# Queries, keys and two head projections as extra Strassen chunks of a feed-forward matrix, and a memory bank padded to 128 rows

## The chip, the core and the metric

The kernel runs on one core of a Trainium2 chip. The metric is the device time of one execution in microseconds (us). Everything is computed in float32.

## What is computed

x has 8 batches of 1024 tokens with 512 features. Cut to what matters:

```python
xn = layernorm(x)                                     # no scale, no shift
# attention block: four heads of 128 features each, joined by warboss_w
def full(xn, w):                                      # local_qkv_w
    q, k, v = split(xn @ w, 3)
    return softmax(q @ k.T * 128 ** -0.5) @ v
def sparse(xn, w):                                    # sparse_qkv_w: the same, but
    keep = scores >= top_k(scores, 102)[..., -1:]     # only the 102 largest of each row stay
    return softmax(where(keep, scores, -1e9)) @ v
def memory(xn):                                       # bank: 64 x 128
    xp = xn @ memory_proj_w                           # 512 -> 128
    r = softmax(xp @ bank.T) @ bank
    return concat([xp, r]) @ mem_out_w + mem_out_b
def prediction(xn):
    h = xn @ pred_in_w + pred_in_b                    # 512 -> 128
    return gelu(h @ pred1_w + pred1_b) @ pred2_w + pred2_b
s = concat([full, sparse, memory, prediction]) @ warboss_w + warboss_b
# feed-forward: 512 -> 2048 -> 512
g = silu(relu(xn @ ffn_w1 + ffn_b1) @ ffn_w2 + ffn_b2)
out = x + s * g
```

## The kernel before

Two streams of work are woven into one order of instructions.

**The filler** is the feed-forward, `feed_forward`. It takes 512 tokens (a *group* g; two to a batch, 16 in all) at a time through ffn_w1 and 256 tokens (n = 2g, 2g+1) through ffn_w2. Both products are done by Strassen's scheme: of a product of 2 x 2 blocks, seven block products in place of eight. ffn_w1 is cut into eight *up chunks* of 512 rows and 2 x 128 columns, ffn_w2 into eight *down chunks*. A chunk holds seven blocks of 128 x 256 (four raw or summed blocks of the weights among them). In the first group a chunk is loaded from the input, its sums are formed (`form_chunk`: four instructions on DVE for up, on POOL for down), and it is written to DRAM; later groups load it from there as one transfer of 896 KB (`load_chunk`). Four tiles w hold chunks; a chunk is loaded three places ahead of its use and formed one place ahead. The order of the chunks is the list that `plan` yields: eight up chunks of a group with down chunks between them, then eight down chunks, the group's *tail*.

The tokens' side of the first product needs sums too: `token_sums` makes four of them per group on POOL from the transposed tokens xnT. An up chunk then is 7 products of two matmuls with 256 columns each (tile ph), copied out of PSUM by ACT into a tile u with seven slots; `hidden_units` adds the seven into the four results on POOL (`add_products`, five instructions) and ACT writes relu of them into h. An up chunk waits until the units two chunks before it are made.

**The attention** works in *steps* of 128 tokens, eight to a batch. It is written as generators (chains), each of which yields a time or a condition: `local` and `sparse` for the two heads, `sparse_select` for the 102 largest scores (DVE: 13 rounds of eight), `two_heads` for the memory and prediction heads of a pair of steps (256 tokens), `finish_pair` for the join with warboss_w.

**The order.** The program's order is made when the kernel is built: `run` keeps an own clock in matmul columns, lets every chain go on whose time or condition has come, and otherwise takes the next matmul of the filler. A new step is started every STEP columns. Every engine executes its instructions in exactly this order (`InOrder`); SP issues the loads, POOL the constants' loads and nearly all stores.

What the change touches is done directly before, by plain matmuls over four row blocks of 128:

- `project_q` makes q of a pair for both attention heads from a resident matrix w_q: 2 x 4 matmuls of 256 columns (tile pq), started by `next_q` in a step of odd number; ACT scales it into qT (one tile).
- `project_k` makes k of a group and a head: 4 matmuls of 512 columns (tile pk), copied by ACT into kT. In batch 0 it is called while the first tokens are prepared; for later batches `project_keys` loads both matrices (`borrow_qkv`) and calls it for two heads and two groups after the last local scores of the batch before.
- `prediction_head` and `memory_head` begin with 4 matmuls of 256 columns each (tiles ppi, pmp) with matrices that `two_heads` loads for each pair (tile wmp, 2 x 256 KB).
- The memory bank has 64 rows. Its scores (pms) have 64 columns; the weights are transposed to 64 rows (ptm), and the second half of the head's product (pmo, from emT and bank_mo) contracts over 64 rows.

All f32 matmuls appear in the profile as two instructions, each with its load of weights.

Of the kernel before, what the change touches and what calls it, by code (L numbers as in the profile page):

```python
# [20 lines left out]
def kernel(  # L21
# [216 lines left out]
    w_q = const.tile([P, ND, 2, HD], F32, tag="w_q", name="w_q")  # L238
    for h in range(2):
        sp.dma_start(out=w_q[:, :, h, :], in_=qkv[h][:, :HD].rearrange("(c p) n -> p c n", p=P))  # L240
# [8 lines left out]
    brow = sb.tile([NB, P], F32, tag="tmp", name="brow", bufs=3)  # L249
# [5 lines left out]
    bank = const.tile([M, HD], F32, tag="bank", name="bank")  # L255
# [10 lines left out]
    bankT = const.tile([P, M], F32, tag="bankT", name="bankT")  # L266
    bank_mo = const.tile([M, HD], F32, tag="bank_mo", name="bank_mo")
# [5 lines left out]
    def turn_constants():  # L273
        pt = ring("pt_b", (P, 4, P))
        transpose(pt[:, 0, :NB], brow, ident[:NB, :NB])
        transpose(pt[:, 1, :M], bank, ident[:M, :M])
        act.copy(biasT, pt[:, 0, :NB])
        copy(bankT, pt[:, 1, :M], 300)
        yield after("act")
        pt = ring("pt_bm", (P, P))  # L280
        matmul(pt[:M, :], bankT, w_mo[:, 1, :], True, True, HD)
        copy(bank_mo, pt[:M, :], 200)
        done.add("constants")
# [55 lines left out]
    def project_k(b, g, h, w):  # L339
        if b not in kT:  # L340
            kT[b] = sb.tile([P, 2, S], F32, tag="kT", name=f"kT_{b}")
        ps = ring(f"pk_{b}_{g}_{h}", (P, 512))
        accumulate(
            ps,
            [w[:, c, ts(h, HD)] for c in range(ND)],
            [xnT[b, g][:, c, :] for c in range(ND)],
            512,
        )
        copy(kT[b][:, h, ts(g, 512)], ps, 360)
        done.add(("k", b, g, h))  # L350
# [18 lines left out]
    def project_q(b, p):  # L369
        qT[b, p] = sb.tile([P, 2, T], F32, tag="qT", name=f"qT_{b}_{p}")  # L370
        ps = ring(f"pq_{b}_{p}", (P, 2, T))
        for h in range(2):
            accumulate(
                ps[:, h, :], [w_q[:, c, h, :] for c in range(ND)], pair_xnT(b, p), T
            )
        act.activation(qT[b, p], ps, AF.Copy, scale=SCALE)
        on("act", 360)
        done.add(("q", b, p))
# [11 lines left out]
    def plan():  # L390


        half = NWC // 2
        for g in range(GROUPS + 1):
            for k in range(NWC):
                if g < GROUPS:
                    yield "up", g, k
                if k >= half and g < GROUPS:
                    yield "down", 2 * g, k - half
                if k < half and g:  # L400
                    yield "down", 2 * g - 1, k + half
            if g < GROUPS:
                for n in range(2):
                    for k in range(half):
                        yield "down", 2 * g + n, k + half * (1 - n)

# [3 lines left out]
        for kind in ("up", "down")  # L410
        for k in range(NWC)
# [3 lines left out]
    w2v = ffn_w2.rearrange("(h k p) n -> p h k n", h=2, p=P)  # L415

# [4 lines left out]
    raw_blocks = sb.tile([P, 7, H], F32, tag="m", name="raw_blocks")  # L421

    def load_chunk(at):
# [5 lines left out]
        if n:  # L429
            sp.dma_start(out=w, in_=w_dram[kind, k])  # L430
            return
        extra = raw[kind, k] = raw_blocks[:, at % 7]
        if kind == "up":
            for slot, u, h in ((0, 0, 0), (1, 0, 1), (4, 1, 1)):
                sp.dma_start(out=halves(w[:, slot]), in_=w1v[:, h, :, u, k])
            sp.dma_start(out=halves(extra), in_=w1v[:, 0, :, 1, k])
        else:
            for slot, h, d in ((0, 0, 0), (1, 1, 0), (6, 1, 1)):
                sp.dma_start(out=w[:, slot], in_=w2v[:, h, k, ts(d, H)])
            sp.dma_start(out=extra, in_=w2v[:, 0, k, H:])  # L440

    def form_chunk(at):

        if at >= len(order_of_chunks) or order_of_chunks[at][1]:
            return
        kind, n, k = order_of_chunks[at]
        w, extra = w_tiles[kind, n, k], raw.pop((kind, k))
        if kind == "up":
# [4 lines left out]
        else:  # L453
            on_pool("tensor_sub", w[:, 5], extra, w[:, 0])
            on_pool("tensor_sub", w[:, 2], w[:, 6], w[:, 5])
            on_pool("tensor_sub", w[:, 3], w[:, 6], extra)
            on_pool("tensor_sub", w[:, 4], w[:, 1], w[:, 2])
        sp.dma_start(out=w_dram[kind, k], in_=w)
# [29 lines left out]
    def token_sums(g):  # L488

        b, q = divmod(g, NG)  # L490
        if g:
            yield needs(("up", g - 1), *[("xnT", b, 4 * q + j) for j in range(4)])
            yield after("act", 0)
        t = sb.tile([P, 4, 2, T], F32, tag="t", name=f"t_{g}")
# [9 lines left out]
    def hidden_units(g, k, m):  # L504
# [3 lines left out]
        for j, slots in enumerate(((1, 4), (6, 5))):  # L508
            h = sb.tile([P, 2, T], F32, tag=f"h{j}", name=f"h_{2 * g + j}_{k}", bufs=(5, NWC)[j])
            for u in range(2):  # L510
                act.activation(h[:, u], m[:, slots[u]], AF.Relu, bias=bcol(k + NWC * u))
                on("act", 280)
            hidden[2 * g + j, k] = h
        units_made[0] += 1

    units_made = [0]
# [40 lines left out]
    def feed_forward():  # L557

        sums = []
        for at, (kind, n, k) in enumerate(order_of_chunks):  # L560
            if kind == "up":
                wants[0] = lambda: (
                    "constants" in done and n in tokens and units_made[0] > n * NWC + k - 2
# [11 lines left out]
            if kind == "up":  # L575
                m = sb.tile([P, 7, T], F32, tag="u", name=f"u_{n}_{k}", bufs=2)
            elif k == NWC - 1:
                m = sb.tile([P, 7, H], F32, tag="m", name=f"m_{n}")
            for i in range(7):
                if kind == "up":  # L580
                    if i % 2 == 0:
                        ps = ring(f"ph_{n}_{k}_{i}", (P, 2, T))
# [20 lines left out]
                if (i % 2 or i == 6) and (kind == "up" or k == NWC - 1):  # L603
                    a = i - i % 2
                    copy(m[:, a : i + 1], ps[:, : i + 1 - a], 180 * (i + 1 - a))
            if kind == "up":
                start(hidden_units(n, k, m), rank=0)
                if k == NWC - 1:
                    tokens.pop(n)
                    done.add(("up", n))  # L610
                    if n + 1 < GROUPS:
                        start(token_sums(n + 1), rank=0)
# [154 lines left out]
    def tmp(name):  # L767
        return sb.tile([P, T], F32, tag="tmp", name=name, bufs=3)

    def memory_head(b, p, w):  # L770
        n = f"{b}_{p}"
        ps = ring(f"pmp_{n}", (P, T))
        accumulate(ps, [w[:, c, :HD] for c in range(ND)], pair_xnT(b, p), T)
        xp = tmp(f"xp_{n}")
        copy(xp, ps, 220)
        yield after("act")
        ps = ring(f"pms_{n}", (P, 2, M))
        for j in range(2):
            matmul(ps[:, j, :], xp[:, ts(j, P)], bankT, True, True, M)
        e = small.tile([P, 2, M], F32, tag="em", name=f"em_{n}", bufs=1)  # L780
# [21 lines left out]
        for j in range(2):  # L802
            transpose(pt[:M, j, :], e[:, j, :], ident)
        eT = tmp(f"emT_{n}")
        copy(eT[:M, :], pt[:M].rearrange("p j t -> p (j t)"), 220)
        yield after("act")
        ps = ring(f"pmo_{n}", (P, T))
        accumulate(ps, [w_mo[:, 0, :], bank_mo[:M, :]], [xp, eT[:M, :]], T)
# [6 lines left out]
    def prediction_head(b, p, w):  # L815
        n = f"{b}_{p}"
        ps = ring(f"ppi_{n}", (P, T))
        accumulate(ps, [w[:, c, HD:] for c in range(ND)], pair_xnT(b, p), T)
        hi = tmp(f"hi_{n}")
        act.activation(hi, ps, AF.Identity, bias=bcol(B_PI))  # L820
        on("act", 260)
        yield after("act")
# [17 lines left out]
    def finish_pair(b, p):  # L840
# [4 lines left out]
        done.add(("borrowed", b, p))  # L845
# [46 lines left out]
    def prepare_tokens(b):  # L892
        yield needs(("rstd", b))
        for j in range(NT):
            if j == 4:
                yield needs(
                    ("up", (b - 1) * NG), ("head", b - 1, 1, 2), ("head", b - 1, 1, 3),
                    *[("up", (b - 1) * NG - 1)] * (b > 1),
                )
# [6 lines left out]

    def project_keys(b):
        yield can_borrow(1)
        w = borrow_qkv(f"wk_{b}", 1)
        yield clock["pe"] + AHEAD  # L910
        yield needs(("local scores", b - 1, NT - 1), ("xnT", b, NT - 1))
        for h in (SPARSE, LOCAL):
            for g in range(NG):
                project_k(b, g, h, w)
                yield clock["pe"] + 700
        give_back()
        project_q(b, 0)
# [14 lines left out]
    def first_tokens():  # L932
# [10 lines left out]
        for g in range(NG):  # L943
# [5 lines left out]
            if g == 0:  # L949
                project_q(0, 0)  # L950
                start(turn_constants())
                start(token_sums(0), rank=0)
                start(hidden_sums(), rank=-1)

    STEP = int(0.98 * (12415 + NWC * (2 * 7 * T + 2 * 7 * H) // 4))
# [9 lines left out]
    for n in range(B * NT):  # L965
# [9 lines left out]
        if i == 4 and b + 1 < B:  # L975
            start(prepare_tokens(b + 1))
        if i % 2:
            if i + 1 < NT:

                def next_q(b=b, p=p):  # L980
                    yield needs(("local scores", b, 2 * p + 1))
                    project_q(b, p + 1)
                    yield 0

                start(next_q(), now + STEP // 4)

            def two_heads(b=b, p=p):
                if (b, p) != (0, 0):
                    yield needs(("borrowed", *divmod(b * NP + p - 1, NP)))
                yield can_borrow(1)  # L990
                w = borrow(f"wmp_{b}_{p}", memory_proj_w, pred_in_w)
                yield clock["pe"] + AHEAD
                yield needs(*before_pair(b, p))
                yield from prediction_head(b, p, w)
                yield from memory_head(b, p, w)
                give_back()
# [3 lines left out]
        if i == NT - 1 and b + 1 < B:  # L1000
            start(project_keys(b + 1), now + 1500)
# [37 lines left out]
```

## Time and profile before

| | |
|---|---|
| median of 3 runs | 2980.77 us (2977.5 to 2980.82) |
| profiled execution: its time | 2975.75 us |
| profiled execution: span from first to last instruction | 2974.0 us |
| granted TensorE clock, mean | 0.998 |
| first matmul starts | 9.73 us after the span's start |
| DMA | 488.32 MB, mean 164 GB/s |
| pq, pk | 512 and 256 instructions |
| ppi, pmp | 256 and 256 instructions |
| ph (up chunks), f (down chunks) | 3584 and 3584 instructions |

The profile is of one execution. PE is TensorE, PEld its weight loads, DVE VectorE, ACT ScalarE, POOL GpSimd, SP the engine that issues loads. All lines show as L85, that of the helper which records every instruction, so groups are told apart by tiles: "out<-in" are the names of the tiles written and read, with buffer numbers left out. Ends of matmuls are modelled, and consecutive ones overlap; the distance of their starts is what a matmul costs in a stream.

### The profile page before, as it was taken

The numbers are of one execution on the slowest core, as the hardware profiler recorded it, in microseconds if no ns is written. First come the engines' busy times: TensorE is split into PE (matmuls) and PEld (weight loads), VectorE is DVE, ScalarE is ACT, GpSimd is POOL, SyncE is SP. The second block draws the span as 40 slices with busy tenths as digits, with TensorE's granted clock in tenths as the row PEclk, the third lists the DMA queues.
The fourth block names the chain that finished last, engine by engine and source line by source line (L and its number), as shares of the span: only waits on it lengthen the run. The fifth ranks groups of instructions, "written<-read, shape, count | busy, mean of one in ns | idle before, by whom it ended". The sixth has DMA issues, their size and how long they took to land.

```text
span 2974.0 us, 36408 instructions
## 1 busy us (share of the span) xinstructions
PE 2923.6 (98%) x12868; PEld 2304.0 (77%) x12868; DVE 2338.7 (79%) x3169; ACT 1549.2 (52%) x2863; POOL 1686.2 (57%) x2244
## 2 busy tenths in 40 slices
PE   8999999999999999999999999999999999999998
PEld 5877777777778777778777887787878778777786
DVE  6998859878698868888599874999839898778771
ACT  3545446554455644655446464465644546355562
POOL 3765626565366564655546654466644666447565
PEclk9999999999999999999999999999999999999999
DMA  5654624545345353454444644445444554434444
GB/s 165 223 208 143 216 98 155 193 139 197 137 161 186 131 191 137 165 181 146 167 149 158 216 138 137 166 173 182 156 157 153 184 175 154 160 110 172 172 152 167
DMA packets 170183, 488.32 MB, mean 164 GB/s; under 512 B 13966, under 2 KB 76448, under 8 KB 170000
## 3 DMA queue, kind: packets, MB, share of 16 engines
q1 hardware_dynamic: 164544, 468.76, 46.1%
q0 software_dynamic: 5456, 17.22, 1.5%
q8 instruction: 102, 1.67, 0.2%
q14 instruction: 81, 0.66, 0.1%
HBM read 454.47 MB, written 31.46 MB: 163 GB/s over the span
## 4 chain that ended last, share of the span: by engine, by line
PE 86%; DVE 7%; ACT 4%; POOL 1%; issue 1%; DMA 1%; SPq 0%; POOLq 0%; DVEq 0%; ACTq 0%
PE f L85 22%; PE ph L85 21%; PE pa L85 7%; PE po L85 7%; PE sc L85 7%; PE pk L85 4%; PE pv L85 4%; PE pq L85 3%; PE ptp L85 3%; DVE top L85 3%; DVE left L85 3%; PE pmp L85 2%; PE pp L85 2%; PE ppi L85 2%; ACT L85 1%; PE pmo L85 1%
## 5 line engine op out<-in xcount | busy, mean ns | idle before, releaser
L85 DVE MAX8 top<-left 128x8 f32<-128x1024 f32 x768 | 943.0, 1228 | 26.7
L85 POOL TENSOR_TENSOR u<-u 128x256 f32<-128x256 f32 (+1 forms) x640 | 619.2, 973 | 478.0 <-ACT u L85 453.4
L85 DVE MATCH_REPLACE8 left<-top,left 128x1024 f32<-128x1024 f32 x704 | 850.7, 1208 | 0.0
L85 PE MATMUL f<-w_down,hs 128*128 128x256 f32 x2048 | 541.5, 380 | 0.8 <-POOL hs L85 0.8
L85 PE MATMUL ph<-t,w_up 128*128 128x256 f32 x2048 | 485.9, 380 | 0.0
L85 POOL TENSOR_TENSOR hs<-h 128x128 f32<-128x128 f32 x512 | 249.4, 487 | 374.9 <-PE f L85 362.8
L85 PEld LDWEIGHTS f<-w_down,hs 128*128 128x128 f32 x2048 | 384.1, 190 | 74.7 <-issue 25.3
L85 PEld LDWEIGHTS ph<-t,w_up 128*128 128x128 f32 x2048 | 381.7, 190 | 63.1 <-issue 15.7
L85 PE MATMUL f<-w_down,h 128*128 128x256 f32 x1536 | 423.7, 380 | 3.7 <-ACT m L85 2.5
L85 PE MATMUL ph<-xnT,w_up 128*128 128x256 f32 x1536 | 387.8, 380 | 1.4 <-ACT u L85 1.4
L85 ACT COPY u<-ph 128x512 f32<-128x512 f32 (+1 forms) x512 | 265.7, 531 | 156.1 <-PE ph L85 155.1
L85 PEld LDWEIGHTS f<-w_down,h 128*128 128x128 f32 x1536 | 286.8, 190 | 54.4 <-issue 13.6
L85 PEld LDWEIGHTS ph<-xnT,w_up 128*128 128x128 f32 x1536 | 285.7, 190 | 50.9 <-issue 13.8
L85 PE MATMUL sc<-kT,qT 128*128 128x512 f32 x512 | 242.6, 595 | 3.7 <-ACT qT L85 3.4
L85 PE MATMUL pa<-pT,v 128*128 128x256 f32 x1024 | 231.3, 379 | 0.0
L85 PE MATMUL po<-wb,head 128*128 128x512 f32 x512 | 230.2, 592 | 0.1
L85 ACT ACTIVATE h<-u,biasT 128x256 f32<-128x256 f32 x512 | 219.1, 501 | 9.5 <-POOL u L85 9.5
L85 DVE MAX8 top<-s 128x8 f32<-128x1024 f32 x64 | 78.2, 1222 | 175.0 <-ACT s L85 175.0
L85 PEld LDWEIGHTS pa<-pT,v 128*128 128x128 f32 x1024 | 194.3, 190 | 27.6 <-issue 1.4
L85 POOL TENSOR_TENSOR o<-o,wb 128x512 f32<-128x512 f32 x64 | 81.6, 1274 | 236.0 <-ACT o L85 236.0
L85 ACT COPY pT<-ptp 128x512 f32<-128x512 f32 x256 | 149.0, 586 | 109.0 <-PE ptp L85 108.1
L85 POOL TENSOR_TENSOR m<-m 128x256 f32<-128x256 f32 (+1 forms) x155 | 147.8, 958 | 56.1 <-ACT m L85 50.9
(120 smaller groups left out, 3766.0 us busy)
## 6 DMA issues: line engine op xcount, KB each, us to landing
w_down<-w_down_dram SPq DMA_DIRECT2D x248, 896.0 KB, 4.7
w_up<-w_up_dram SPq DMA_DIRECT2D x120, 896.0 KB, 4.6
wb<-in_L_attn_warboss_w_dram SPq DMA_DIRECT2D x64, 512.0 KB, 6.4
xl<-in_L_attn_x_dram SPq DMA_DIRECT2D x64, 256.0 KB, 4.7
xr<-in_L_attn_x_dram SPq DMA_DIRECT2D x64, 256.0 KB, 3.3
out_dram<-xr POOLq DMA_DIRECT2D x62, 256.0 KB, 2.8
xs<-in_L_attn_x_dram SPq DMA_DIRECT2D x56, 256.0 KB, 4.9
wmp<-_attn_memory_proj_w_dram SPq DMA_DIRECT2D x32, 256.0 KB, 2.9
```

The costliest lines, as they stand in the source:

```text
L85: r = made(*args, **kwargs)
```

## The change

- `plan` yields new kinds of chunks: "q" and "k", which are the query and key columns of the local and the sparse matrix (128 + 128 columns), and "m", which is memory_proj_w and pred_in_w side by side. Each is one chunk of the same form as an up chunk: seven products, four results. "m" stands in each group after the third up chunk; the q of a group stands in the tail of the group before; the k of both groups of a batch, and the q of its first, stand in the tail of the batch before (the second group's k first, then the sums of the first group's tokens, its k and its q).
- q and k of batch 0 are not needed as chunks at once (its k, and the q of its first group, are still made directly), so an entry "form" only loads, forms and stores them, in the first group.
- `token_sums` of a batch's second group are made twice: once for its k (t_k), once for the rest.
- `use_units` takes the place of `hidden_units` and treats the four results by kind: relu into h, a scaled write into qT, a copy into kT, or a copy and a biased write into a new tile xh that the two heads start from. The first waits in it are those on the local scores that still read the old qT or kT, and, for m, on the heads of the group before.
- qT and xh have two buffers, tmp two in place of three. w_q, the loads wmp and those of later batches' keys go; pair 1's q is made directly beside pair 0's.
- The bank's transposes and products are padded to 128 rows or columns with zeros (`bankT`, `weights`, `bank_mo`); the scores and the softmax keep 64 columns.
- The tokens of the next batch are prepared from step 3 on in place of 4, with other conditions. STEP's factor and constant change.

The core of the diff:

```diff
 def plan():
                 if k < half and g:
                     yield "down", 2 * g - 1, k + half
+                if k == 2 and g < GROUPS:
+                    yield "m", g, 0
+                if g == 0 and k in (3, 5):
+                    yield "form", "qk"[k // 4], 0
             if g < GROUPS:
                 for n in range(2):
                     for k in range(half):
                         yield "down", 2 * g + n, k + half * (1 - n)
+                        if g + 1 < GROUPS:
+                            at = n * half + k
+                            if (g + 1) % NG == 0:
+                                if at == 2:
+                                    yield "k", g + 2, 0
+                                if at == 5:
+                                    yield "k", g + 1, 0
+                                    yield "q", g + 1, 0
+                            elif at == 3:
+                                yield "q", g + 1, 0
...
+    def blocks(kind, k):
+        if kind == "up":
+            return [w1v[:, :, :, u, k] for u in range(2)]
+        if kind == "m":
+            ws = memory_proj_w, pred_in_w
+        else:
+            ws = [w[:, ts("qk".index(kind), HD)] for w in qkv]
+        return [w.rearrange("(h c p) n -> p h c n", h=2, p=P) for w in ws]
...
+    SLOTS = ((1, 4), (6, 5))
+    def use_units(kind, g, k, m, nth):
         for _ in add_products(m, on_pool):
             yield pool_is_free
         yield after("pool")
...
+        elif kind == "q":
+            yield needs(("local scores", b - (q == 0), (4 * q - 1) % NT))
+            for pair, slots in zip(pairs, SLOTS):
+                make_q(*pair)
+                for u in range(2):
+                    act.activation(qT[pair][:, u], m[:, slots[u]], AF.Copy, scale=SCALE)
+                    on("act", 230)
+                done.add(("q", *pair))
+        elif kind == "k":
+            yield needs(("local scores", b - 1, NT - 1))
+            make_k(b)
+            for (_, p), slots in zip(pairs, SLOTS):
+                for u in range(2):
+                    copy(kT[b][:, u, ts(p, T)], m[:, slots[u]], 230)
+            for u in range(2):
+                done.add(("k", b, q, u))
+        else:
...
+            for pair, slots in zip(pairs, SLOTS):
+                t = sb.tile([P, 2, T], F32, tag="xh", name=f"xh_{pair[0]}_{pair[1]}", bufs=2)
+                copy(t[:, 0], m[:, slots[0]], 230)
+                act.activation(t[:, 1], m[:, slots[1]], AF.Identity, bias=bcol(B_PI))
...
+        done.add(("units", nth))
...
 def feed_forward():
+            if kind == "form":
+                wants[0] = lambda: True
+                yield 0
+                load_chunk(at + 3)
+                form_chunk(at + 1)
+                w_tiles.pop((kind, n, k))
+                continue
...
 def memory_head(b, p, xp):
-        ps = ring(f"pmp_{n}", (P, T))
-        accumulate(ps, [w[:, c, :HD] for c in range(ND)], pair_xnT(b, p), T)
-        xp = tmp(f"xp_{n}")
-        copy(xp, ps, 220)
-        yield after("act")
...
-        e = small.tile([P, 2, M], F32, tag="em", name=f"em_{n}", bufs=1)
+        e = weights[:, :, :M]
...
-            transpose(pt[:M, j, :], e[:, j, :], ident)
+            transpose(pt[:, j, :], weights[:, j, :], ident)
...
-        accumulate(ps, [w_mo[:, 0, :], bank_mo[:M, :]], [xp, eT[:M, :]], T)
+        accumulate(ps, [w_mo[:, 0, :], bank_mo], [xp, eT], T)
...
-    STEP = int(0.98 * (12415 + NWC * (2 * 7 * T + 2 * 7 * H) // 4))
+    STEP = int(0.995 * (12031 + NWC * (2 * 7 * T + 2 * 7 * H) // 4))
...
             def two_heads(b=b, p=p):
-                yield can_borrow(1)
-                w = borrow(f"wmp_{b}_{p}", memory_proj_w, pred_in_w)
-                yield clock["pe"] + AHEAD
-                yield needs(*before_pair(b, p))
-                yield from prediction_head(b, p, w)
-                yield from memory_head(b, p, w)
-                give_back()
+                yield needs(("m", b, p), *before_pair(b, p))
+                t = starts.pop((b, p))
+                yield from prediction_head(b, p, t[:, 1])
+                yield from memory_head(b, p, t[:, 0])
```

## The prediction

> **What bounds the kernel now.** I read the busy shares first, then the chain that ended last, then the chain in order of time for what one matmul costs in a stream, then PE's waits, and last the timeline where the change works.
>
> ```profile
> PE 2923.6 (98%) x12868; PEld 2304.0 (77%) x12868; DVE 2338.7 (79%) x3169; ACT 1549.2 (52%) x2863; POOL 1686.2 (57%) x2244
> PE 86%; DVE 7%; ACT 4%; POOL 1%; issue 1%; DMA 1%; SPq 0%; POOLq 0%; DVEq 0%; ACTq 0%
> ```
>
> PE is busy all the time and carries 86% of the chain. A matmul's end is modelled, so busy time alone proves little; the spacing in the chain does (start, duration, what):
>
> ```profile
> 370.58 3.45 PE pa L85 x16
> 1962.86 6.04 PE ph L85 x28
> 2185.23 6.04 PE f L85 x28
> ```
>
> One f32 matmul is two instructions; every 256-column instruction takes 3.45/16 = 6.04/28 = 216 ns, whatever its operands. PE runs at its issue rate, so the time is the number of columns sent through it, plus its waits.
>
> Rule and row must be weighed here. The Trainium skill (Perfetto Trace Analysis, "Identifying the Most-Contended Engine") says that matmul occupancy is no measure of a busy TensorE and that the LDWEIGHTS share is. By it PE stands at 77% and has slack, and a removal of matmuls could bring down to nothing. But a load here takes 190 ns under a matmul of 216 ns, and 430 ns for 512 columns: a gapless stream can't show more than 88%. Start-to-start spacing decides: gapless. I take the full value of removed columns; by the rule it could be 0.
>
> ```profile
> PE sc L85 <- ACT qT L85: 3.4, 5, 0.7
> PE f L85 <- ACT m L85: 2.5, 1, 2.5
> ```
>
> PE's waits (us, times, longest) are small; these two lie where the change works. Here is one of the five, at a batch boundary:
>
> ```profile
> 375.60 3.60 PE L85 MATMUL pk<-xnT,wk 128*128 128x512 f32 x8
> 379.04 1.03 PE L85 MATMUL pp<-hi,w_p 128*128 128x256 f32 x4
> ...
> 400.16 3.62 PE L85 MATMUL pq<-xnT,w_q 128*128 128x256 f32 x16
> 404.46 1.98 PE L85 MATMUL sc<-kT,qT 128*128 128x512 f32 x4 [0.69 <-ACT qT L85]
> ```
>
> Eight pk instructions take 379.04 - 375.60 = 3.44 us (430 ns for 512 columns). Sixteen pq take 3.45 and should end at 403.61; sc starts at 404.46, so 0.85 us is lost.
>
> **The change, part by part.**
>
> *Direct matmuls removed.* pq: 30 of 32 pairs, 30 x 3.45 = 103.5 us. pk: 28 of 32 blocks, 28 x 3.44 = 96.3. ppi and pmp: 64 x 8 instructions, 512 x 0.216 = 110.6. Sum 310.4 us, all in PE's stream.
>
> *Chunks added.* 15 of q, 14 of k, 16 of m, each 7 products x 2 row blocks x 2 instructions = 28, like an up chunk: 45 x 6.04 = 271.8 us. Net **-38.6 us**. In columns: a group loses 3 x 2 x 256, a 128-token step 384, which is what the constant in STEP falls by.
>
> *Bank padded to 128 rows.*
>
> ```profile
> 2944.88 0.59 PE L85 MATMUL pmo<-xp,w_mo 128*128 128x256 f32 x2
> 2945.40 0.70 PE L85 MATMUL pmo<-emT,bank_mo 64*128 64x256 f32 x2
> 2946.03 0.70 PE L85 MATMUL f<-w_down,h 128*128 128x256 f32 x2
> 2946.56 1.03 PE L85 MATMUL f<-w_down,hs 128*128 128x256 f32 x4
> ```
>
> A pair of instructions should take 0.43 us from start to start. The pair before the 64-row one takes 0.52, the 64-row pair 0.63, the pair after it 0.53: 1.68 for 1.30, 0.38 us lost, 32 times: **-12.3 us**. The Trainium skill would say 0: TensorE: Matmul & The Clock Gate, "Why this matters for your kernels", gives a matmul of few rows the time of one with 128. The row decides; the mechanism that fits it is in TensorEngine Tiling (Array Packing), "Key Properties": a change of tiling mode drains the engine. The transposes of 64 columns (ptm) are spaced like other transposes, about 110 ns, and I give their padding nothing.
>
> *Waits at the boundary.* The pq-to-sc wait goes: -5 x 0.85 = -4.2 us. But q now comes by PE, ACT (copy out), POOL (five adds), ACT (scale): 0.37 + 4.87 + 4 x 0.501 (the row of h<-u, 128x256) = 7.2 us if nothing stands in these queues. In the order of after.py 22 to 40 matmuls (9.5 to 17 us) lie between the last q product and the first scores of a batch, 22 to 24 in the last four batches, and the hidden sums of two or three "down" chunks (4 x 0.48 us each) stand in POOL's queue there. PE is in order: while sc waits, everything behind it waits. And by the generator's own rules a unit is done when its last ACT instruction is issued, not finished. Bounds: 0, and 2.0 us (the four ACT instructions) at each of 7. I take 1.5 at 4 boundaries: **+6.0** (0 to 14).
>
> *First group.* m, q and k are formed: 12 DVE instructions of about 760 ns = 9.1 us, and pair 1's q moves ahead of the first scores, 3.45 us later for the top-k. The cover is thin: DVE is 92.35 of 99 us busy at 99 to 198 us, and the 2.5 us "f <- ACT m" stems from it (ACT stood at a square root that waited for DVE's statistics, and m's copies behind it). Bounds 0 and 12.6; I take **+3.0**. Below nothing is possible too if the few idle places of PE there (some 8 us between 154 and 175) are filled; I don't count on it.
>
> *POOL.*
>
> ```profile
> L85 POOL TENSOR_TENSOR u<-u 128x512 f32<-128x512 f32 x256 | 331.6, 1296 | 354.5 <-ACT u L85 346.1
> L85 POOL TENSOR_TENSOR u<-u 128x256 f32<-128x256 f32 x384 | 291.0, 758 | 123.5 <-ACT u L85 107.3
> ```
>
> A chunk's sums: 2 x 1.296 + 3 x 0.758 = 4.87, x 45 = 219 us; the second token sums of 7 batches, 28 x 1.3 = 36. 1686 becomes 1942, 66% of the span. The two memsets lie in POOL's idle 8.7 us before its first token sum. Hidden, since units are read two chunks later (12 us of PE at least); if POOL falls behind by more than that, "ph" or "f" waits next.
>
> *ACT.* Out of PSUM 45 x (3 x 0.583 + 0.373) = 95.5; 92 scaled or biased halves x 0.501 = 46.1; 88 copies x 0.373 = 32.8; 5 more table loads x 1.28 = 6.4. Gone: qT 17.9, kT 16.4, hi 15.2, xp 11.9. Net +119 us, 57%. Hidden, as long as PSUM tiles are emptied in time: PE waited 1.4 us for that in all.
>
> *SP and the DMAs.* 44 more reloads of 896 KB, 3 writes and 12 small loads, less 78 of 256 KB: about +24 MB on 488. A reload lands in 4.7 us and is issued three chunks ahead (18 us of PE); a form-only entry in between leaves two (12). SP waits in order for the buffer's last matmul, so x and output-weight loads behind it keep their place; they are wanted thousands of columns later. Taken as nothing; bound above, 45 x 1 us. The earlier call of the token preparation moves x loads, DVE and 32 transposes of a batch ahead by one step, no work more.
>
> *Sum.* -38.6 - 12.3 - 4.2 + 6.0 + 3.0 = -46.1 us. I add +1 for ACT and POOL arriving later now and then: -45. The profiled execution has a span of 2974.0 and a time of 2975.75, 5.0 under the median of 2980.77; taken off the median: **2936 us**.
>
> **The rivals.**
>
> *A, the sum holds* (0.74): -33 to -62 us, 2919 to 2948. It reaches its low end where the +9 don't show and boundaries close up.
>
> *B, half comes back as waits* (0.19). For it: the detour by POOL and ACT is new at 15 q and 14 k chunks, and ACT and POOL are in order. Against: PE's waits behind the up chunks, which make the same detour 128 times, are below 3 us in all. Price: 29 x 0.8 = 23 us, so -22: 2959, between 2948 and 2970.
>
> *C, POOL at the batch boundary* (0.04), slower. The token sums of the second group, its k, then the first group's sums again (the same tile, so only after that k), k and q form a chain: 5.2 + 4.9 + 2.0 = 12 us per boundary if none is hidden, 7 x 12 = 85, giving -51 + 85 = +34: 3015. It decides from 7.3 us per boundary (51/7). Against it: POOL is only about 40% busy there (365 to 464 us: 37.1 of 99) and 14 to 28 "down" matmuls stand between the links.
>
> *D, PE does not shorten* (0.03): the weight load, not the columns, sets the pace, as the 77% rule would have it; the padding's 12 us then goes into the new waits. 2981, within 6.
>
> **How the numbers follow.** Predicted 2936. Range 2918 to 2960: A whole and the near half of B, which leaves out some 0.2. 0.2% is 6 us, about what a measurement of this kernel tells from no change. Faster: A and B, 0.93; same: D, 0.03; slower: C, 0.04.
>
> **What would show it.** Right: "ph" with k, q and m at 28 instructions in 6.04 us; pq, pk at 16 and 32 instructions; no 64-row matmul, and pmo with its neighbours at 0.43 us a pair; PE still 98% of the span; POOL near 1940 us, ACT near 1670; a row "PE sc <- ACT qT" of 3 to 8 us. Wrong: PE's waits (mainly on ACT u, qT, kT or POOL) above 40 us in all would be B or C; the padding is misjudged if pmo pairs stay above 0.5 us; the form step, if PE waits over 12 us more before 200 us.

## The result: 26 us less, and the profile after

| | before | after |
|---|---|---|
| median of 4 runs each | 2979.14 us | 2953.14 us (2950.7 to 2955.75) |
| ratio, 95% interval | | 0.9913 (0.9896 to 0.993) |
| span of the profiled execution | 2974.0 us | 2951.1 us |

The change takes off 26.0 us (21 to 31 by the interval) where 45 were forecast. The two profiled executions differ by 22.9 us in their spans. The page of the profile after, busy shares and chain:

```profile
PE 2881.2 (98%) x12912; PEld 2322.4 (79%) x12912; DVE 2369.6 (80%) x3181; ACT 1641.4 (56%) x3106; POOL 1937.4 (66%) x2499
PE 81%; DVE 8%; ACT 5%; POOL 2%; DMA 1%; issue 1%; SPq 0%; POOLq 0%; DVEq 0%; ACTq 0%
```

PE is still 98% of the span. POOL has grown to what was worked out (1937 us, 1942 forecast). ACT stands at 1641 us where about 1670 were forecast: the durations of its instructions sum to 117 us more, as worked out (119), but more of them overlap, and its busy time grew by 92. But PE's part of the chain has fallen from 86 to 81%: DVE, ACT and POOL now end more of its steps. The chain in order of time shows what the new chunks cost:

```profile
716.70 6.04 PE ph_k L85 x28
1844.86 6.04 PE ph_q L85 x28
2444.98 6.04 PE ph_m L85 x28
```

28 instructions in 6.04 us, as an up chunk has. The timeline of PE at the last padded product:

```profile
2917.21 0.60 PE L85 MATMUL pmo<-xh,w_mo 128*128 128x256 f32 x2
2917.64 0.60 PE L85 MATMUL pmo<-emT,bank_mo 128*128 128x256 f32 x2
2918.08 0.60 PE L85 MATMUL f<-w_down,hs 128*128 128x256 f32 x2
2918.51 1.03 PE L85 MATMUL f<-w_down,h 128*128 128x256 f32 x4
```

The three distances of starts are 0.43, 0.44 and 0.43 us, where they were 0.52, 0.63 and 0.53. So both gains are there in full. What was lost beside them shows first in PE's waits (us in all, times, longest):

```profile
PE ptx L85 <- DVE xl L85: 19.0, 14, 9.7
PE pp L85 <- ACT xh L85: 11.1, 12, 1.4
PE pk L85 <- ACT xnT L85: 3.7, 2, 3.2
PE ptm L85 <- DVE weights L85: 3.6, 6, 1.1
PE f L85 <- POOL w_down L85: 3.1, 1, 3.1
...
PE sc L85 <- ACT qT L85: 0.4, 2, 0.2
```

All rows of this view sum to 40.8 us before and 59.6 after. "pp <- xh" is new; "ptx <- xl" was 12.8 us in 6 waits. (The 9.7 of ptx is the start of the kernel, in both.)

A wait costs more than its idle time, since the first matmul behind it comes late too. I therefore add up, from the start times of the trace, how much later every matmul starts than the usual distance behind the one before it (216 ns for 256 columns, 429.5 for 512, 109 for 128, 90 for 64, 120 for what is left):

| us, profiled executions | before | after |
|---|---|---|
| usual distances, summed | 2892.0 | 2853.6 |
| late starts, summed | 62.5 | 78.0 |
| of these at pp | 0.0 | 15.8 |
| at ptx | 5.9 | 14.2 |
| at ptp | 10.7 | 8.8 |
| at pmo | 7.9 | 0.0 |

-38.3 of columns and +15.5 of late starts make -22.8, and the spans differ by 22.9. Within the 15.5, padding took away 12.4: the two instructions of each 64-row product and the two behind them started about 93, 104, 90 and 104 ns late, 0.39 us in all, 32 times. Of this 6.3 lay at pmo (the rest of its 7.9 is one wait for ACT) and 6.1 at the matmuls behind. Then pp brought 15.8, ptx 8.3 and all others together 3.8. So without the padding's part the late starts rose by 27.9 us (from 50.1 to 78.0), where the prediction had put 5.8 (-4.2 + 6.0 + 3.0 + 1).

### The profile page after: what moved, and what is told of

Same layout as the page of the kernel before. It is cut to its first block, busy times and chain, and to the rows that moved or that the text cites. A ratio compares the mean times of both kernels' runs of the same rounds, so it can differ in the third digit from the quotient of the medians.

```text
span 2951.1 us, 37099 instructions
## 1 busy us (share of the span) xinstructions
PE 2881.2 (98%) x12912; PEld 2322.4 (79%) x12912; DVE 2369.6 (80%) x3181; ACT 1641.4 (56%) x3106; POOL 1937.4 (66%) x2499
## 4 chain that ended last, share of the span: by engine, by line
PE 81%; DVE 8%; ACT 5%; POOL 2%; DMA 1%; issue 1%; SPq 0%; POOLq 0%; DVEq 0%; ACTq 0%
PE ph_up L85 22%; PE f L85 21%; PE pa L85 7%; PE po L85 7%; PE sc L85 6%; PE pv L85 4%; PE ptp L85 3%; DVE top L85 3%; DVE left L85 3%; PE ph_m L85 3%; PE ph_k L85 2%; PE ph_q L85 2%; PE pp L85 1%; ACT L85 1%; ACT h L85 1%
## 5 line engine op out<-in xcount | busy, mean ns | idle before, releaser
L85 POOL TENSOR_TENSOR u_up<-u_up 128x256 f32<-128x256 f32 (+1 forms) x640 | 619.9, 974 | 329.9 <-ACT u_up L85 304.5
L85 PE MATMUL ph_up<-t,w_up 128*128 128x256 f32 x2048 | 483.2, 380 | 0.0
L85 PEld LDWEIGHTS f<-w_down,hs 128*128 128x128 f32 x2048 | 383.9, 191 | 71.0 <-issue 18.8
L85 PEld LDWEIGHTS ph_up<-t,w_up 128*128 128x128 f32 x2048 | 385.1, 191 | 65.2 <-issue 17.9
L85 ACT COPY u_up<-ph_up 128x512 f32<-128x512 f32 (+1 forms) x512 | 264.1, 530 | 238.3 <-PE ph_up L85 237.4
L85 PE MATMUL ph_up<-xnT,w_up 128*128 128x256 f32 x1536 | 383.3, 380 | 1.1 <-ACT el L85 0.9
L85 PEld LDWEIGHTS ph_up<-xnT,w_up 128*128 128x128 f32 x1536 | 288.3, 191 | 45.2 <-issue 8.1
L85 ACT ACTIVATE h<-u_up,biasT 128x256 f32<-128x256 f32 x512 | 219.7, 501 | 8.4 <-POOL u_up L85 8.4
L85 POOL TENSOR_TENSOR m<-m 128x256 f32<-128x256 f32 (+1 forms) x155 | 152.1, 989 | 64.0 <-ACT m L85 59.6
```

Of the source, the lines that this page charges most:

```text
L85: r = made(*args, **kwargs)
```

## The experiments

Theory 1: the missing gain went into PE standing at pp. The removed head starts (ppi, pmp) each had a wait for ACT behind them in the planner (`yield after("act")`). Now `use_units` calls the unit done when its ACT instructions are issued, `two_heads` goes on in the same moment, and PE meets pp before ACT has written xh. Theory 2: ACT and POOL are fuller, and the waits would turn up somewhere in any case.

**e1: the heads wait for ACT.**

```diff
                 yield needs(("m", b, p), *before_pair(b, p))
+                yield after("act")
                 t = starts.pop((b, p))
```

> The changed kernel, with one line more: the two heads of a pair start only when the planner's clock says that ACT is through with what it has been given (the write of xh among it). Theory 1 (the gain that is missing went into PE standing at pp for xh, because the unit is called done when its ACT instructions are issued): the row 'PE pp <- ACT xh' (11.1 us, 12 times) falls under 3 us, and the time by 9 to 16 us. Theory 2 (PE's new waits come from ACT and POOL being fuller, and only show at pp because it is the first in the queue): the row falls but other rows behind ACT grow by as much, and the time stays within 4 us.

Measured: 2940.29 us (2938.56 to 2945.08), ratio to before 0.9874 (0.9861 to 0.9888), 12.9 us less than the changed kernel. The row "pp <- xh" is gone, and the late starts at pp fall from 15.8 to 1.5 us, of all matmuls from 78.0 to 65.5. Its first rows of PE's waits:

```profile
PE ptx L85 <- DVE xl L85: 19.4, 10, 10.2
PE pk L85 <- ACT xnT L85: 4.0, 2, 3.5
PE ptm L85 <- DVE weights L85: 3.1, 6, 0.8
```

Theory 1 holds for this term: of the 14.3 us that went at pp, 12.5 are gone from the sum of all late starts; only some 2 us came back elsewhere. One of the waits in the changed kernel, ACT and PE, shows how it arose:

```profile
1730.65 1.15 ACT L85 ACTIVATE el<-el,r_l 128x1024 f32<-128x1024 f32 x1
1731.70 0.59 PE L85 MATMUL ph_up<-xnT,w_up 128*128 128x256 f32 x2
1731.90 0.58 ACT L85 COPY u_up<-ph_up 128x512 f32<-128x512 f32 x1
1732.38 0.41 ACT L85 COPY xh<-u_m 128x256 f32<-128x256 f32 x1
1732.69 0.51 ACT L85 ACTIVATE xh<-u_m,biasT 128x256 f32<-128x256 f32 x1
...
1733.25 1.13 PE L85 MATMUL pp<-xh,w_p 128*128 128x256 f32 x4 [0.95 <-ACT xh L85]
```

PE has issued its matmuls up to about 1732.1; xh stands in ACT's order behind a normalization and a copy, and PE, in order itself, can do nothing else.

**e2: the padding alone**, on the kernel before (its core; the bank's own tile also moves into a buffer of tmp, to make room):

```diff
-            transpose(pt[:M, j, :], e[:, j, :], ident)
+            transpose(pt[:, j, :], weights[:, j, :], ident)
...
-        accumulate(ps, [w_mo[:, 0, :], bank_mo[:M, :]], [xp, eT[:M, :]], T)
+        accumulate(ps, [w_mo[:, 0, :], bank_mo], [xp, eT], T)
```

> The kernel before, with the bank's transposes and products padded to 128 rows and nothing else of the change. By the spacing of the 64-row rows of the trace (0.38 us lost, 32 times): 12 us less than before, no pmo pair over 0.44 us. By the rule that few rows cost as much as 128: no change, within 3 us.

Measured: 2968.39 us against 2978.96, ratio 0.9967 (0.9955 to 0.9979): 10.6 us less (6 to 13). The row was right. What the Trainium skill says in TensorE: Matmul & The Clock Gate, "Why this matters for your kernels" (a single matmul of 32 rows takes the time of one with 128) does not give the cost here, where 64-row products stand singly between full ones and delay the matmul behind them too. In this run the 12.4 us are gone from their places, and 4 us of other late starts came in (54.2 in all); the last padded product:

```profile
2936.61 0.59 PE L85 MATMUL pmo<-xp,w_mo 128*128 128x256 f32 x2
2937.04 0.59 PE L85 MATMUL pmo<-emT,bank_mo 128*128 128x256 f32 x2
2937.47 0.59 PE L85 MATMUL f<-w_down,h 128*128 128x256 f32 x2
```

**e3: the old pace.**

```diff
-    STEP = int(0.995 * (12031 + NWC * (2 * 7 * T + 2 * 7 * H) // 4))
+    STEP = int(0.98 * (12031 + NWC * (2 * 7 * T + 2 * 7 * H) // 4))
```

> The changed kernel with the factor of STEP put back from 0.995 to 0.98, so that the attention's steps start 1.5% more often against the filler. Theory 1 (the waits at pp and ptx stand in the code's missing ACT wait and in DVE's queue): 'PE pp <- ACT xh' stays between 7 and 15 us, and the time is 0 to 8 us longer, since more of the last steps lies without filler beside it. Rival (the pace, not the chunks, made PE's new waits): the waits on ACT xh and DVE xl fall by half and the time by about 8 us.

Measured: 2951.1 us (2948.73 to 2953.64): no difference from the changed kernel that these runs can tell. The waits changed places:

```profile
PE pp L85 <- ACT xh L85: 13.2, 12, 4.0
PE ptx L85 <- DVE xl L85: 12.5, 6, 9.4
PE sc L85 <- ACT qT L85: 7.9, 8, 1.9
```

The wait at pp stays at this pace too, which the rival excluded. That at ptx does depend on the pace, as the rival had it (late starts 6.8 us in place of 14.2), but most of what it gives is taken back elsewhere: at sc late starts rose from 6.8 to 12.5 us, at ph_up from 2.2 to 8.2, and all of them fell only from 78.0 to 75.4. Between these two paces the waits changed places more than their sum. The 7.9 us of "sc <- qT" is, by the way, what the prediction had feared for the changed kernel (3 to 8), and there it was 0.4.

**e4: the tokens' transposes later.**

```diff
         on("dve", 330)
-        return after("dve")
+        return after("dve", 2000 if b else SLACK)
```

> The changed kernel, with the transposes of the next batch's tokens issued 1600 columns (2.7 us) of the planner's clock later after DVE's normalization (batches 1 to 7). If the 19.0 us of 'PE ptx <- DVE xl' is DVE being late behind its top-k rounds (2.5 us each) against what the planner assumes: that row falls to the 10 to 11 us of the start and the time by 6 to 9 us. If the wait is only a symptom of a fuller kernel: the wait moves to other rows, and the time stays within 3 us.

Measured: 2948.46 us (2947.77 to 2949.83), 4.7 less than the changed kernel. Its first rows:

```profile
PE pp L85 <- ACT xh L85: 12.3, 10, 2.3
PE ptx L85 <- DVE xl L85: 10.6, 2, 9.4
PE ptp L85 <- ACT es L85: 5.1, 3, 4.3
```

The ptx row fell to that of the start, and the late starts at ptx from 14.2 to 4.3 us. But those at ptp rose from 8.8 to 17.1, so of ten us less than half was kept (all late starts: 78.0 to 74.1). This is between the two expectations: DVE was late, and part of the wait moved on.

**e5: both edits (e1 and e4).**

> Both edits that took time off the changed kernel, together: the two heads wait for ACT, and the tokens' transposes come 1600 columns later. If the two waits are separate, the gains add: -13 and -5 against the changed kernel's 2953, so about 2935, 44 us less than before, which is the sum of the prediction. If PE's waits are one pool that moves from row to row, the second edit adds nothing: 2940.

Measured: 2935.12 us, ratio 0.9853 (0.9838 to 0.9867), and once more beside e7 2935.61 us, ratio 0.9858 (0.9844 to 0.9871). The gains add, and this version beats both kernels: 43 to 44 us under the kernel before, near the 45 of the prediction's sum. Its first rows:

```profile
PE ptx L85 <- DVE xl L85: 11.3, 2, 9.8
PE ptp L85 <- ACT es L85: 4.3, 4, 2.1
PE pk L85 <- ACT xnT L85: 3.9, 2, 3.3
PE pp L85 <- ACT h L85: 3.2, 2, 1.7
```

Late starts are 60.8 us in this profiled execution and 64.5 in the second one. That is about the 62.5 of the kernel before, but 12.4 of those came from the 64-row products; against the other 50.1, some 11 to 14 us of new late starts are left.

**e6: k's weights formed in the second group**, on top of e5:

```diff
-                if g == 0 and k in (3, 5):
+                if (g, k) in ((0, 3), (1, 5)):
...
-        extra = raw_blocks[:, at % 7]
+        extra = w[:, 3] if (kind, n) == ("form", "k") else raw_blocks[:, at % 7]
```

> The same, with k's weights formed in the second group in place of the first (their raw block goes into a slot of the chunk's own tile). If the forming of q, k and m in the first group costs PE time by way of DVE (92 of 99 us busy there), as the prediction's term of +3 has it: 1 to 4 us less than the run with both edits, and fewer waits before 210 us ('ph_up <- DVE w_up' of 2.9 us goes). If it was hidden: within 1 us.

Measured: 2938.45 us (2934.68 to 2940.17). It doesn't help; against e5's 2935 it is rather longer, within its own spread. The "ph_up <- DVE w_up" row fell from 3.0 to 1.6 us, so forming does reach PE by way of DVE, but the order of everything behind it changed too and gave back more (late starts at ptp: 18.8 us, 11.0 in e5). The prediction's term of 3 us for forming is neither shown nor excluded by this.

**e7: the heads direct again**: the changed kernel without m chunks. One thing more differs: the second half of a batch's tokens waits again for two heads of the batch before, as in the kernel before the change.

```diff
-                if k == 2 and g < GROUPS:
-                    yield "m", g, 0
...
-                yield needs(("up", (b - 1) * NG), ("v", b - 1))
+                yield needs(
+                    ("up", (b - 1) * NG), ("v", b - 1),
+                    ("head", b - 1, 1, 2), ("head", b - 1, 1, 3),
+                )
...
-                yield needs(("m", b, p), *before_pair(b, p))
-                t = starts.pop((b, p))
...
+                w = borrow(f"wmp_{b}_{p}", memory_proj_w, pred_in_w)
...
+                accumulate(ps, [w[:, c, HD:] for c in range(ND)], pair_xnT(b, p), T)
+                act.activation(t[:, 1], ps, AF.Identity, bias=bcol(B_PI))
+                yield after("act")
                 yield from prediction_head(b, p, t[:, 1])
+                accumulate(ps, [w[:, c, :HD] for c in range(ND)], pair_xnT(b, p), T)
+                copy(t[:, 0], ps, 220)
+                yield after("act")
                 yield from memory_head(b, p, t[:, 0])
```

> The changed kernel without its m chunks: the two heads start from direct matmuls again (ppi, pmp, each followed by a wait for ACT as before); q and k stay chunks, the padding stays. PE gets 110.6 - 96.7 = 13.9 us of columns back. If the m chunks lost as much by the wait at pp (15.8 us of late starts at pp) as they saved, as built they were worth nothing: the time is within 5 us of the changed kernel's 2953, while its row 'PE pp <- ACT xh' is gone. If the missing time sits with q and k (POOL and ACT fuller, batch boundaries), the waits stay and the time is 10 to 16 us longer: about 2966.

> The run with both edits once more on this chip, beside the direct heads, as their common measure: 2935, 43 to 45 us under the kernel before. If e7 is at 2953, the m chunks with the wait in its place and the tokens later are worth 18 us.

Measured: 2959.33 us (2957.93 to 2960.55), ratio 0.9936 (0.9922 to 0.995). That is 6.2 us more than the changed kernel, which lies between the two expectations. PE has 13.8 us of columns more (2867.5 for 2853.6), and its late starts are 70.7 us in place of 78.0. The waits at pp and most of those at ptx are gone, but others came:

```profile
PE ptx L85 <- DVE xl L85: 9.9, 1, 9.9
PE sc L85 <- ACT qT L85: 5.6, 7, 1.2
PE ptp L85 <- ACT es L85: 4.3, 3, 2.1
PE pk L85 <- ACT xnT L85: 4.2, 2, 3.7
PE ph_up L85 <- ACT u_up L85: 4.0, 1, 4.0
```

So as built the m chunks, together with tokens that need not wait for these heads, brought 6 us where their columns are 14. The difference to e5 is 23.7 us, more than these columns, so e7 does not single out what the m chunks are worth. And q and k as chunks bring late starts of their own: 70.7 us here against 54.2 with the padding alone (e2). Some of theory 2, and of the prediction's rival B, is true there, only not for the pp term, which e1 took away nearly whole.

## Why the prediction came out as it did

The case forecast as likeliest was that the sum holds (-33 to -62 us). What came, -26, is rival B's: the mechanism was right, and waits ate part of it. By the steps:

- *PE's columns*: forecast -38.6, measured -38.3. Chunks at 28 instructions in 6.04 us, direct matmuls at their spacing: the row held. PE's load share rose from 77 to 79%, and the time fell with the columns all the same, so the rule that would have allowed 0 for them is not what bounds here. (The page that the prediction names for it asks for the share of peak FLOP/s beside the load share, as measures of headroom; the prediction took the load share alone.) One number in its list was a slip: pq stands at 32 instructions after the change, not 16, as its own 30 of 32 pairs says.
- *Padding*: forecast -12.3, measured -10.6 alone (e2), the 0.38 us per product gone in the rows (12.4 in the late starts). The drain named as the mechanism fits and isn't shown by itself.
- *Waits at the boundary*: -4.2 came about (3.4 us of "sc <- qT" became 0.4). The +6.0 for new ones there did not: from the last q product to the next scores PE had at least 22 matmuls (9.7 us) to do, more than the 7.2 that the detour was put at. e3 shows that this depends on the order: 7.9 us there.
- *First group*: forecast +3.0. Late starts in the first 200 us rose from 16.0 to 20.8, +4.7, but they are 18.5 in e2 too, which leaves this stage nearly as it was. The largest new one is not DVE's forming but "f <- POOL w_down" (3.1 us): on POOL the second group's token sums (146.5 to 152.5 us) stand ahead of the down chunk's forming.
- *ACT and POOL*: POOL's busy time and ACT's added work were right, and the size given to their effect on PE, +1, is the step that failed. In its place stood 15.8 us at pp and 8.3 at ptx. The prediction listed what ACT has to do, and that the first steps of both heads go; it did not list that two `yield after("act")` went with them, and these had kept pp away from an ACT result not yet written. So the loss at pp is not that ACT was too full; PE was sent there too early (e1). It had even noted, for q, that a unit is done when issued, and costed it only there. Where it named what would show B, "PE's waits above 40 us in all", it set the mark where the kernel before already stood (40.8).
- *Rival B's price* (29 detours of q and k at 0.8 us, 23 us) came near in sum, in part by luck: in the changed kernel most of the waits lie at the m chunks' users and at the token transposes, which it did not name. Waits behind q show in e3 and e7 ("sc <- qT" 7.9 and 5.6 us).
- *Rivals C and D* did not come: no wait on POOL at a batch boundary stands among PE's rows.

Open: how much of the wait at ptx comes from the tokens being prepared one step earlier. The part of DVE being held up by POOL can be bounded (below), and it is the smaller one.

## What to carry to other kernels

When an edit takes away an instruction, look also for the wait that stood behind it: what it protected may now meet its input unfinished, and on an in-order engine that costs the time of all that is queued behind. In a planner with its own clock, "issued" and "done" are two things; one line that lets the consumer wait was worth half as much as the whole change. And the gain in columns on a gapless engine came in exactly here; what had to be estimated is the late starts, and they can be counted from the distance of starts, before and after.

## What the hardware showed that was not expected

Some DVE instructions stand still while POOL works. The instruction that scales the memory weights (tile em before, weights after; min, median and max in ns):

```profile
L85 DVE TENSOR_SCALAR em<-em,rm x64: 241/254/1301, 126.1 to 2942.1; 128x64 f32<-128x64 f32 x64
```

```profile
L85 DVE TENSOR_SCALAR weights<-weights,rm x64: 240/491/1362, 115.9 to 2910.2; 128x64 f32<-128x64 f32 x64
```

Same work, same shortest time, the median nearly doubled. From the start times: 46 of the 64 are over 100 ns above the shortest after the change (17 before). After the change every one of them started while a POOL tensor instruction was running, and all but one end 48 to 57 ns after that one's end. The selection's last step (es, 128x1024) behaves likewise, 1457 ns on average before and 1589 after, its slow ones ending mostly 1.08 us after POOL's. The selection's rounds do not: MAX8 (1195 to 1230 ns) and MATCH_REPLACE8 (1198 to 1214) vary by less than 40 ns. Such waiting for the other's end fits the exclusive lock that the Trainium skill describes for the port pair that VectorE and GpSimd share (SBUF — State Buffer, "Who interferes with whom"); that these instructions use that pair no run here shows. POOL's load alone does not set how often they meet: in e7 POOL is busy for 1863 us (1686 before, 1937 after) and the median of this instruction is 254 ns again. Such a case in front of PE, in the timeline of the changed kernel (POOL, DVE, PE):

```profile
1292.11 2.13 POOL L85 TENSOR_TENSOR u_q<-u_q 128x512 f32<-128x512 f32 x2
1292.24 1.42 DVE L85 TENSOR_SCALAR xl<-xl,mv,rs 128x512 f32<-128x512 f32 x1
...
1293.80 0.41 PE L85 MATMUL ptx<-ident,xl 128*128 128x128 f32 x2 [0.63 <-DVE xl L85]
```

The normalization of 0.57 us (its median) takes 1.42; POOL had begun on q's sums 0.13 us earlier, and the transposes then wait. So POOL's 251 us of added work were not quite hidden: they lengthen some of DVE's instructions, and with them what PE waits for. At ptx this is the smaller part. Behind the first batch 15 of its late starts are over 0.1 us and sum to 12.1 us; what their normalizations took above 545 ns (the median before) makes 4.3 at most. At five of them (4.7 us) the normalization took its usual time and had only begun late, at four of these directly behind a MAX8 of the selection, which agrees with e4.
